# One-hots of a graph layer, made four tiles at a time with the tile as the inner dimension

## The chip, the cores and the metric

The kernel runs on one core of one Trainium2 chip. The metric is device microseconds of one execution, as the median of several runs; lower is better. Engines are called as the profile calls them: PE (TensorE matmul), PEld (TensorE weight load), DVE (VectorE), ACT (ScalarE), POOL (GpSimd) and SP (SyncE).

## The reference, cut to what matters

Two graph layers over 6250 nodes with 128 features and 106250 edges (100000 drawn, and one from each node to itself), sorted by `dst`:

```python
h = relu(layernorm(x));  x = x + L0(h)          # L0: degree-normalised sum over neighbours
h = relu(layernorm(x));  x = x + L1(h)          # L1: attention over the edges, by src
# L0
xw = h @ W;  deg = segment_sum(ones, dst);  dinv = rsqrt(deg)
out = relu(segment_sum(xw[src] * (dinv[src] * dinv[dst])[:, None], dst) + b)
# L1
att = exp(clip(sum_d(q[src] * k[dst]) / 4, -10, 10))     # 8 heads of 16
out = segment_sum(att * v[dst], src) / segment_sum(att, src);  layernorm(out + h) * gamma + beta
...
```

The first layer sums by `dst`, the order in which the edges come. The second one sums by `src`, so the kernel has to sort the edges by `src` on the chip, which it does beside the work of the first layer.

## The kernel before, in words

128 edges make a tile, one edge on each partition; there are `EC` = 831 tiles. Nodes are in `NB` = 49 blocks of 128.

**Head** (to about 110 us): layer norm of all nodes, degrees, `xw` scaled by `dinv`, written to the table `gtab`.

**First layer** (about 110 to 1065 us). The tiles come in groups of four (`G0`). For each group POOL gathers the rows of `gtab` by index (`gather`, L397, tile `gt`, 5 buffers), DVE makes a one-hot of the places within a window of 64 nodes (L923), PE sums by it (L952, `ps`), and DVE adds to `acc` (L934). When a block's edges are done, `finish0` adds, normalises and projects it. The first 16 blocks (`PC`) go another way: their edges are counted per pair of nodes, which gives a dense matrix `counts`, and `product` (L795) multiplies that with `xwp`, three bf16 parts of `xw`.

Between the groups stands the other work, by two lists of steps with written-out costs; `beside(k)` takes from each until its share for group k is spent. Engines then run their instructions in the order in which these were issued. The lists hold:

- `count_pair` (L756): two windows of 128 edges of the dense blocks. DVE compares a row of slot numbers with a code per edge, 245 columns (L769, `win_oh`, 4 buffers of a pair each), one instruction for each window. `put_counts` (L776) multiplies a pair two pairs later: 416 matmuls of 245 columns (L780), whose moving operand is `win_oh` and whose weights are `win_ol`; ACT copies the result (L783).
- the sort: keys, ranks (L550 to L553), positions; up to about 620 us.
- `place(t)` (L627), for each of the 831 tiles, about 623 to 1065 us: it puts the edges of tile t into their sorted places. DVE makes lane one-hots for 8 tiles at once, with the tiles as the inner dimension (`lanes`, L622 and L624, tile `ol`, 2 buffers). ACT scales one tile's lane one-hot (L641, `ola`, `LAG + 4` buffers); for one in four groups of 8, DVE does it (L635, `ola_v`). DVE compares slot numbers with a code, over the cells that tile t can reach (L643, `oh_tau`, `LAG + 4` buffers), one instruction per tile:

```python
oh = l0.tile([P, CELLS_IN * NB], F16, name="oh_tau", bufs=LAG + 4)
nc.vector.tensor_scalar(oh[:, :(hi + 1 - lo) * NB], self.slot16[:, lo * NB:(hi + 1) * NB],
                        r["code"][:, t:t + 1], None, op0=OP.is_equal)
```

`window(t)` gives the cells lo to hi; a cell is 49 columns. From its formula 133 tiles have one cell, 183 two, 116 three, 138 four, 200 five and 61 six. `put` (L650), `LAG` = 6 tiles later, multiplies: twice the tile's columns (weights `ol` and `ola`, moving operand `oh_tau`), in one or two pieces each (L656, `pp`).

- `unpack`, `rows_of` (L660, tile `lt`, 4 buffers) and flags, up to about 1105 us.

**Second layer** (from about 1110 us): attention over the sorted edges, block by block. The change doesn't touch it.

Of the kernel before, what the change touches and what calls it, by code (L numbers as in the profile page):

```python
# [7 lines left out]
F32 = mybir.dt.float32  # L8
F16 = mybir.dt.float16
BF16 = mybir.dt.bfloat16  # L10
I32 = mybir.dt.int32
# [3 lines left out]
OP = mybir.AluOpType  # L15
# [6 lines left out]
P = 128  # L22
D = 128
# [10 lines left out]
G1 = 3  # L34
BT = 16
PT = 8
LAG = 6
PC = 16
CN = 5
CW = -(-P // CN)  # L40
# [12 lines left out]
class Kernel:  # L53
# [31 lines left out]
    def setup(self, early):  # L85
        self.early = early
        nc, tc, ctx, NB, N = self.nc, self.tc, self.ctx, self.NB, self.N
# [7 lines left out]
        for name, a in (("dst", self.dstp), ("src", self.srcp)):  # L95
            t = self.nodes.tile([P, self.ER + 1], I32, name=f"{name}_i", tag=f"rows_{name}")
# [52 lines left out]
        nc.gpsimd.iota(pid_i, pattern=[[P, 2]], base=0, channel_multiplier=1)  # L149
        self.pid = const.tile([P, 2], F32, name="pid")  # L150
        nc.scalar.copy(self.pid, pid_i)
        NS = 1024
        slot_f = hp.tile([P, NS], F32, name="slot_f")
        nc.gpsimd.iota(slot_f, pattern=[[1, NS]], base=0, channel_multiplier=0,
                       allow_small_or_imprecise_dtypes=True)
# [2 lines left out]
        self.slot16 = const.tile([P, NS], F16, name="slot16")  # L158
        nc.scalar.copy(self.slot16, slot_f)

        self.lanes = self.nodes.tile([P, P, PT], F16, name="lanes")
        nc.scalar.copy(self.lanes, self.slot_f[:, :P, None].to_broadcast([P, P, PT]))

# [237 lines left out]
    def layer0(self):  # L401
        nc, tc, NB, NP, N, E, EC, ER, ET = self.nc, self.tc, self.NB, self.NP, self.N, self.E, self.EC, self.ER, self.ET
# [16 lines left out]
        with ExitStack() as l0c:  # L419
            l0k = l0c.enter_context(tc.tile_pool(name="l0k", bufs=1))  # L420
            l0 = l0c.enter_context(tc.tile_pool(name="l0", bufs=2))
            fin = l0c.enter_context(tc.tile_pool(name="fin", bufs=3))
# [61 lines left out]
            r = {}  # L484
# [118 lines left out]
            def window(t):  # L603
                per_tile = P * N / E
                d0, d1 = t * per_tile, (t + 1) * per_tile
                d0, d1 = d0 - 16 - 1.6 * d0 ** 0.5, d1 + 16 + 1.6 * d1 ** 0.5
                if d1 < PB * P:
                    return max(int(d0), 0) // (2 * P), int(d1) // (2 * P)
                share = (E - N) / N * P / N
                most = max(d1 - PB * P, 0) * share  # L610
                least = max(d0 - PB * P, 0) * share * min(1.0, self.LAST / P)
                hi = CELLS + min(int(most + 4.5 * most ** 0.5) // P, FAR - 1)
                if d0 < PB * P:
                    return max(int(d0), 0) // (2 * P), hi
                return CELLS + max(int(least - 4.5 * least ** 0.5), 0) // P, hi

            placed = []
            CELLS_IN = max(hi + 1 - lo for lo, hi in map(window, range(EC)))

            def lanes(t0, n):  # L620
                r["ol"] = l0.tile([P, 2, P, PT], F16, name="ol", bufs=2)
# [5 lines left out]
            def place(t):  # L627
                lo, hi = window(t)
                on_vector = t // PT % 4 == 3
                if t % PT == 0:  # L630
                    n = min(PT, EC - t)
                    lanes(t, n)
                    if on_vector:
                        r["ola"] = l0.tile([P, P, PT], F16, name="ola_v", bufs=1)
                        nc.vector.tensor_tensor(r["ola"][:, :, :n], r["ol"][:, 0, :, :n],  # L635
                                                r["a16"][:, None, t:t + n].to_broadcast([P, P, n]), op=OP.mult)
                if on_vector:
                    ola = r["ola"][:, :, t % PT]
                else:
                    ola = l0.tile([P, P], F16, name="ola", bufs=LAG + 4)  # L640
                    nc.scalar.activation(ola, r["ol"][:, 0, :, t % PT], AF.Copy, scale=r["a"][:, t:t + 1])  # L641
                oh = l0.tile([P, CELLS_IN * NB], F16, name="oh_tau", bufs=LAG + 4)
                nc.vector.tensor_scalar(oh[:, :(hi + 1 - lo) * NB], self.slot16[:, lo * NB:(hi + 1) * NB],  # L643
                                        r["code"][:, t:t + 1], None, op0=OP.is_equal)
                placed.append((t, lo, hi, oh, r["ol"], ola))
                if len(placed) > LAG:
                    put()
# [12 lines left out]
            def rows_of(table, what, c, m):  # L660
                pt, k = bank()
                nc.tensor.transpose(pt[:m, :P], what[:, c:c + m], self.ident)
                lt = fin.tile([P, P], BF16, name="lt", bufs=4)
                nc.scalar.copy(lt[:m, :], pt[:m, :P])
                let_go(k)
                nc.sync.dma_start(table[c:c + m, :], lt[:m, :])
# [60 lines left out]
            wins = {}  # L727

            def fetch_windows(q):
                rows = l0.tile([P, 2, P], I32, name="win", bufs=2)  # L730
                m = CQ * CW
                nc.gpsimd.indirect_dma_start(
                    out=rows[:m].rearrange("p a b -> p (a b)"), out_offset=None, in_=self.wins,
                    in_offset=bass.IndirectOffsetOnAxis(ap=self.win_row[:m, q:q + 1], axis=0))
                ints = l0.tile([P, 2, P], I32, name="win_int", bufs=1)
                nc.vector.tensor_scalar(ints[:m, 0, :], rows[:m, 0, :], 7, None, op0=OP.arith_shift_right)
                nc.vector.tensor_scalar(ints[:m, 1, :], rows[:m, 0, :], P - 1, None, op0=OP.bitwise_and)

                val = l0.tile([P, 2, P], F32, name="win_val", bufs=1)
                nc.vector.tensor_scalar(val[:m, 0, :], rows[:m, 1, :], self.win_node[:m, q:q + 1], float(NB),  # L740
                                        op0=OP.subtract, op1=OP.mult)
                nc.vector.tensor_tensor(val[:m, 0, :], val[:m, 0, :], ints[:m, 0, :], op=OP.add)
                nc.vector.tensor_copy(val[:m, 1, :], ints[:m, 1, :])
                pt, k = bank()
                for i in range(2):
                    nc.tensor.transpose(pt[:, i * P:i * P + m], val[:m, i, :], self.ident[:m, :m])
                code = l0.tile([P, P], F32, name="win_code", bufs=2)
                nc.scalar.copy(code[:, :m], pt[:, :m])
                lane = l0.tile([P, P], F16, name="win_lane", bufs=2)
                nc.scalar.copy(lane[:, :m], pt[:, P:P + m])  # L750
                let_go(k)
                wins[q] = [code, lane]

            counted = []

            def count_pair(b, j):  # L756
                q, m = b // CQ, CQ * CW
                code, lane = wins[q]
                w0 = b % CQ * CW + 2 * j
                oh = l0.tile([P, 2, 256], F16, name="win_oh", bufs=4)  # L760
                ols = []
                for h in range(2):
                    w = w0 + h
                    if w % PT == 0:
                        n = min(PT, m - w)
                        wins["ol"] = l0.tile([P, P, PT], F16, name="win_ol", bufs=2)
                        nc.vector.tensor_tensor(wins["ol"][:, :, :n], self.lanes[:, :, :n],
                                                lane[:, None, w:w + n].to_broadcast([P, P, n]), op=OP.is_equal)
                    nc.vector.tensor_scalar(oh[:, h, :CN * NB], self.slot16[:, :CN * NB], code[:, w:w + 1], None,  # L769
                                            op0=OP.is_equal)  # L770
                    ols.append(wins["ol"][:, :, w % PT])
                counted.append((j, oh, ols))
                if len(counted) > 2:
                    put_counts()

            def put_counts():  # L776
                j, oh, ols = counted.pop(0)
                cb = cbps.tile([P, 512], F32, name="cb")
                for h in range(2):
                    nc.tensor.matmul(cb[:, h * CN * NB:(h + 1) * CN * NB], ols[h], oh[:, h, :CN * NB], start=True,  # L780
                                     stop=True)
                c0 = 2 * j * CN
                nc.scalar.copy(self.counts[:, c0:c0 + 2 * CN, :].rearrange("p n b -> p (n b)"), cb[:, :2 * CN * NB])  # L783
# [60 lines left out]
            loads = {}  # L844

            def load0(b):
                own = fin.tile([P, D], F32, name="own", bufs=4)
                nc.sync.dma_start(own, gtab_v[:, b, :])
                xs = fin.tile([P, 1, D], F32, name="xs0", bufs=4)
                if b < NB - 1:  # L850
                    nc.sync.dma_start(xs[:, 0, :], self.x[b * P:(b + 1) * P, :])
                else:
                    nc.vector.memset(xs, 0.0)
                    nc.sync.dma_start(xs[:self.LAST, 0, :], self.x[b * P:N, :])
                loads[b] = own, xs
# [62 lines left out]
            ohs, sums, ats = {}, {}, {}  # L918
# [22 lines left out]
            for g in range(GA, self.NG0):  # L941
                n = size[g]
# [630 lines left out]
```

## Time and profile before

| what | value |
|---|---|
| median of 9 runs | 2329.36 us (2318.76 to 2342.37) |
| profiled execution, its own time | 2318.62 us |
| its span | 2316.8 us |
| PE, DVE, ACT, POOL busy | 73%, 67%, 43%, 52% |
| granted clock of PE, mean | 0.788 |

The profiled execution is one of the quicker ones: its own time is 10.7 us below the median. A stage is read as a stretch of the span; `win_oh` is made from 112.8 to 644.4 us, `oh_tau` from 623.0 to 1062.7 us. A mean duration counts an instruction from its start to its end; the next one on the same engine often starts before that, so the distance between starts is what an engine pays.

### The profile page before, as it was taken

The page shows a single profiled execution, that of the slowest core. Times are in us where ns is not written, and L with a number is a line of the kernel's source. Part 1 is how long each engine was busy: PE and PEld are TensorE (multiplying, and loading weights), DVE is VectorE, ACT ScalarE, POOL GpSimd, SP SyncE. Part 2 cuts the span into 40 slices and gives each one's busy share as a digit, 9 for nine tenths or more (in the row PEclk, how much of TensorE's full clock was granted, in tenths as well). Part 3 has the DMA queues.
Part 4 walks back from the last instruction along what each step waited for, and adds up shares of the span by engine and source line. Part 5 has one row for each costly group of instructions (what it writes and reads, how often), then busy time and mean ns, then how long its engine had stood idle before and what let it go on. Part 6 is the DMA issues. An engine that isn't in the chain of part 4 may idle for free.

```text
span 2316.8 us, 42149 instructions
## 1 busy us (share of the span) xinstructions
PE 1693.1 (73%) x14638; PEld 1440.2 (62%) x14638; DVE 1545.7 (67%) x4956; ACT 985.4 (43%) x2782; POOL 1193.8 (52%) x1173
## 2 busy tenths in 40 slices
PE   4335778877778888886448777777787777777777
PEld 4324667766666676565337666676676676676666
DVE  7822588778658888895236666567666667667667
ACT  6642443333347767772113343334334334334234
POOL 0575324554556666777455445454544554544550
PEclk9556787878765577996568788889888888888888
DMA  4411122222222222222634335334434434433440
GB/s 91 106 48 50 54 71 74 72 76 65 62 71 58 61 59 61 60 63 64 217 107 123 116 104 156 105 121 140 138 110 136 126 125 131 134 112 117 121 123 17
DMA packets 157205, 222.72 MB, mean 96 GB/s; under 512 B 30494, under 2 KB 115343, under 8 KB 156983
## 3 DMA queue, kind: packets, MB, share of 16 engines
q0 software_dynamic: 47488, 118.69, 18.0%
q1 hardware_dynamic: 103147, 98.05, 13.8%
q10 hardware_dynamic: 6348, 3.20, 0.7%
q8 instruction: 117, 1.92, 0.3%
q14 instruction: 105, 0.86, 0.1%
HBM read 192.44 MB, written 27.39 MB: 95 GB/s over the span
## 4 chain that ended last, share of the span: by engine, by line
PE 59%; issue 14%; DVE 9%; ACT 7%; another core or an unknown queue 5%; DMA 3%; POOL 1%; DVEq 0%; SPq 0%; ACTq 0%; POOLq 0%
PE po L1078 13%; PE pk L1036 11%; PE pq L1046 9%; PE cb L795 8%; PE pp L656 5%; PE ps L952 5%; PE ot L1050 3%; ACT ola L641 2%; PE cb L780 2%; DVE oh_tau L643 2%; ACT counts L783 2%; PE ps_f L890 1%; POOL gt L397 1%; DMA gt<-gtab,idx 1%
## 5 line engine op out<-in xcount | busy, mean ns | idle before, releaser
L397 POOL DMA_INDIRECT gt<-gtab,idx x567 | 609.6, 1075 | 491.2 <-issue 147.2
L397 POOL DMA_INDIRECT kv<-kvtab,idx x588 | 574.6, 977 | 558.6 <-DVE ohD L1029 173.6
L1046 PE MATMUL pq<-qb,ohT 128*128 128x128 bf16 x2940 | 262.3, 229 | 111.4 <-issue 106.7
L1036 PE MATMUL pk<-kvp,ohD 128*128 128x256 bf16 x2205 | 307.6, 293 | 24.5 <-issue 20.2
L1052 ACT COPY oh<-ot 128x384 f32<-128x384 f32 (+1 forms) x343 | 157.8, 463 | 353.7 <-PE pq L1046 98.1
L641 ACT ACTIVATE ola<-ol,a_f 128x128 f16<-128x128 f16 x624 | 272.1, 520 | 72.6 <-DVE ol L622 28.9
L1046 PEld LDWEIGHTS <-ohT 128*128 128x128 bf16 x2940 | 212.1, 103 | 138.2 <-issue 127.9
L952 PE MATMUL ps<-oh,gt 128*128 128x64 f32 x1134 | 216.9, 348 | 82.7 <-DVE acc L934 30.2
L1036 PEld LDWEIGHTS <-ohD 128*128 128x128 bf16 x2205 | 230.1, 105 | 71.8 <-issue 33.5
L952 PEld LDWEIGHTS ps<-oh,gt 128*128 128x128 f32 x1134 | 204.8, 265 | 92.0 <-issue 51.3
L795 PE MATMUL cb<-xwp,counts 128*128 128x128 bf16 x2352 | 194.0, 254 | 37.2 <-issue 28.4
L656 PE MATMUL pp<-oh_tau,ol 128*128 128x49 f16 (+5 forms) x947 | 198.5, 268 | 30.7 <-issue 11.6
L795 PEld LDWEIGHTS <-counts 128*128 128x128 bf16 x2352 | 187.5, 155 | 46.6 <-issue 39.1
L1058 DVE TENSOR_TENSOR pr<-pq,kv 128x384 f32<-128x384 f32 x196 | 108.6, 554 | 154.8 <-PE pk L1036 50.2
L643 DVE TENSOR_SCALAR oh_tau<-slot,code 128x245 f16<-128x245 f16 (+5 forms) x831 | 178.0, 277 | 24.2 <-PE pp L656 16.9
L1060 DVE TENSOR_REDUCE att<-pr 128x24 f32<-128x384 f32 x343 | 187.2, 546 | 0.1
L783 ACT CAST counts<-cb 128x490 bf16<-128x490 f32 x208 | 113.2, 570 | 169.5 <-PE cb L780 118.1
L1039 ACT COPY kvn<-pk 128x512 f32<-128x512 f32 (+1 forms) x245 | 115.6, 496 | 159.4 <-PE pq L1046 54.0
L1064 ACT ACTIVATE ex<-att 128x24 f32<-128x24 f32 x343 | 76.7, 224 | 228.8 <-DVE att L1062 152.6
L1029 DVE TENSOR_SCALAR ohD<-dr,pid 128x384 bf16<-128x384 bf16 (+1 forms) x294 | 81.6, 310 | 126.3 <-PE ot L1050 57.1
L656 PE MATMUL pp<-oh_tau,ola 128*128 128x98 f16 (+5 forms) x716 | 153.1, 261 | 15.6 <-issue 1.3
L1050 PE MATMUL ot<-identb,ohT 128*128 128x128 bf16 x980 | 125.8, 232 | 49.2 <-issue 41.9
(1766 smaller groups left out, 3131.7 us busy)
## 6 DMA issues: line engine op xcount, KB each, us to landing
lr<-lrow SPq DMA_DIRECT2D x48, 640.0 KB
dr<-drow SPq DMA_DIRECT2D x48, 256.0 KB
kv<-kvtab,idx POOLq DMA_INDIRECT x588
gt<-gtab,idx POOLq DMA_INDIRECT x567
kvtab<-kvout SPq DMA_DIRECT2D x49, 128.0 KB
kvn<-kvtab SPq DMA_DIRECT2D x49, 128.0 KB
qtab<-qp SPq DMA_DIRECT2D x49, 96.0 KB
qb<-qtab SPq DMA_DIRECT2D x48, 96.0 KB
```

Of the source, the lines that this page charges most:

```text
L397: self.nc.gpsimd.indirect_dma_start(out=to, out_offset=None, in_=table, in_offset=bass.IndirectOffsetOnAxis(ap=idx[:, t:t + 1], axis=0))
L641: nc.scalar.activation(ola, r["ol"][:, 0, :, t % PT], AF.Copy, scale=r["a"][:, t:t + 1])
L643: nc.vector.tensor_scalar(oh[:, :(hi + 1 - lo) * NB], self.slot16[:, lo * NB:(hi + 1) * NB], r["code"][:, t:t + 1], None, op0=OP.is_equal)
L656: nc.tensor.matmul(pp[:, h, (x0 - f0) * NB:(x1 - f0) * NB], o, oh[:, (x0 - lo) * NB:(x1 - lo) * NB], start=False, stop=t == EC - 1, skip_g ...
L783: nc.scalar.copy(self.counts[:, c0:c0 + 2 * CN, :].rearrange("p n b -> p (n b)"), cb[:, :2 * CN * NB])
L795: nc.tensor.matmul(prods[b][:, :D], self.counts[:, :P, k], self.xwp[:, k, x, :], start=(k, x) == (0, 0), stop=(k, x) == (NB - 1, 2))
L952: nc.tensor.matmul(ps, gt[:, j, :], oh[:, j, :], start=(j == 0), stop=(j == n - 1))
L1036: nc.tensor.matmul(pk[:, i - c, :], ohD[:, h, i * P:(i + 1) * P], kvp[:, 2 * tiles[i] + h, x, :], start=(h, x) == mine[0], stop=(h, x) == ...
L1046: nc.tensor.matmul(pq[:, i * D:(i + 1) * D], left, qb[:, x * D:(x + 1) * D], start=(x == 0), stop=(x == 2))
L1050: nc.tensor.matmul(ot[:, i, :], ohT[:, i * P:(i + 1) * P], identb, start=True, stop=True)
L1060: nc.vector.tensor_reduce(att[:, :n * H], pr[:, :n, :].rearrange("p g (h d) -> p (g h) d", h=H), axis=AX.X, op=OP.add)
L1078: nc.tensor.matmul(po, left, wv_[:, i, :], start=(k == 0 and i == 0), stop=(k == len(steps) - 1 and i == n - 1))
```

## The change

Both wide one-hots are made for `PW` = 4 tiles by one comparison of two tensors. The constant `wide` holds each slot number four times side by side; the tile is the inner dimension of the result, so that one tile's columns stand 4 f16 elements (8 bytes) apart. That strided view is now the moving operand of the matmuls. For the places, the codes are first made relative to the first cell of the four tiles (`rel_code`), whose cells are the union of the four windows. `LAG` goes from 6 to 4 (so `ola` has 8 buffers), and some pools have fewer buffers (`lt`, `win`, `own`, `xs0`), which makes room in SBUF.

```diff
-LAG = 6
+PW = 4
+LAG = 4
...
+        self.wide = self.nodes.tile([P, CW5, PW], F16, name="wide")
+        nc.scalar.copy(self.wide, slot_f[:, :CW5, None].to_broadcast([P, CW5, PW]))
...
-                oh = l0.tile([P, CELLS_IN * NB], F16, name="oh_tau", bufs=LAG + 4)
-                nc.vector.tensor_scalar(oh[:, :(hi + 1 - lo) * NB], self.slot16[:, lo * NB:(hi + 1) * NB],
-                                        r["code"][:, t:t + 1], None, op0=OP.is_equal)
+                if t % PW == 0:
+                    n = min(PW, EC - t)
+                    r["lo"], last = window(t)[0], window(t + n - 1)[1]
+                    cols = (last + 1 - r["lo"]) * NB
+                    rel = l0.tile([P, PW], F16, name="rel_code", bufs=3)
+                    nc.vector.tensor_scalar(rel[:, :n], r["code"][:, t:t + n], -float(r["lo"] * NB), None, op0=OP.add)
+                    r["oh"] = l0.tile([P, CELLS_IN * NB, PW], F16, name="oh_tau", bufs=3)
+                    nc.vector.tensor_tensor(r["oh"][:, :cols, :n], self.wide[:, :cols, :n],
+                                            rel[:, None, :n].to_broadcast([P, cols, n]), op=OP.is_equal)
+                oh = r["oh"][:, (lo - r["lo"]) * NB:(hi + 1 - r["lo"]) * NB, t % PW]
...
-                lt = fin.tile([P, P], BF16, name="lt", bufs=4)
+                lt = fin.tile([P, P], BF16, name="lt", bufs=2)
...
-                rows = l0.tile([P, 2, P], I32, name="win", bufs=2)
+                rows = l0.tile([P, 2, P], I32, name="win", bufs=1)
...
+                nc.vector.tensor_scalar(val[:m, 0, :], val[:m, 0, :], -1.0, 1024.0, op0=OP.max, op1=OP.min)
...
-                code = l0.tile([P, P], F32, name="win_code", bufs=2)
+                code = l0.tile([P, P], F16, name="win_code", bufs=2)
...
-                oh = l0.tile([P, 2, 256], F16, name="win_oh", bufs=4)
...
-                    nc.vector.tensor_scalar(oh[:, h, :CN * NB], self.slot16[:, :CN * NB], code[:, w:w + 1], None,
-                                            op0=OP.is_equal)
+                    if w % PW == 0:
+                        n = min(PW, m - w)
+                        wins["oh"] = l0.tile([P, CN * NB, PW], F16, name="win_oh", bufs=2)
+                        nc.vector.tensor_tensor(wins["oh"][:, :, :n], self.wide[:, :CN * NB, :n],
+                                                code[:, None, w:w + n].to_broadcast([P, CN * NB, n]), op=OP.is_equal)
+                    ohs.append(wins["oh"][:, :, w % PW])
...
-                    nc.tensor.matmul(cb[:, h * CN * NB:(h + 1) * CN * NB], ols[h], oh[:, h, :CN * NB], start=True,
+                    nc.tensor.matmul(cb[:, h * CN * NB:(h + 1) * CN * NB], ols[h], ohs[h], start=True,
...
-                own = fin.tile([P, D], F32, name="own", bufs=4)
+                own = fin.tile([P, D], F32, name="own", bufs=3)
-                xs = fin.tile([P, 1, D], F32, name="xs0", bufs=4)
+                xs = fin.tile([P, 1, D], F32, name="xs0", bufs=3)
```

## The prediction

> **What bounds the kernel now.** I read the chain of waits by stages first, then the busy time by stages. The chain from 183 to 623 us (counts, products, sort) lists PE L795 at 39.4%, L780 at 7.7% and L952 at 8.7%, and DVE's L769 at 3.1%. From 860 to 1065 us (the wide places) it lists PE L656 at 32.9%, and on DVE L643 at 14.8% and L622 and L624 at 7.4% and 6.4%.
>
> ```profile
> 183.00:623.00 440.00, 335.24 (x2990) 286.65 (x2991) 302.94 (x947) 166.10 (x414) 207.51 (x199) 0.78 0.24 66
> 623.00:860.00 237.00, 191.53 (x1585) 156.85 (x1583) 176.65 (x714) 156.97 (x388) 148.96 (x139) 0.60 0.23 62
> 860.00:1065.00 205.00, 172.84 (x1202) 125.95 (x1202) 181.28 (x680) 146.30 (x358) 146.08 (x130) 0.89 0.22 60
> ```
>
> The columns are length, busy PE, PEld, DVE, ACT, POOL, granted clock, DMA share, GB/s. In the last stage DVE is busy 88% and PE 84%: two engines stand near their end. The change takes work from DVE, and gives PE another way of reading. So the price of both has to be found, by bursts in the timeline and by the tiles' rows:
>
> ```profile
> 43.15 1.73 PE L289 MATMUL ps_b<-hi,lo 128*128 128x49 f16 x16
> 1002.98 1.53 DVE L643 TENSOR_SCALAR oh_tau<-slot,code 128x294 f16<-128x294 f16 x7
> 856.80 1.28 DVE L643 TENSOR_SCALAR oh_tau<-slot,code 128x147 f16<-128x147 f16 x7
> 720.49 1.10 DVE L643 TENSOR_SCALAR oh_tau<-slot,code 128x49 f16<-128x49 f16 x7
> L289 PE MATMUL ps_b<-hi,lo x96: 253/280/287, 43.2 to 58.5; 128*128 128x49 f16 x96
> L282 DVE TENSOR_TENSOR hi<-lanes,nblk x6: 561/567/569, 40.2 to 53.0; 128x784 f16<-128x784 f16 x6
> L286 DVE TENSOR_TENSOR lo<-lanes,nlane x6: 1218/1220/1222, 40.7 to 53.5; 128x2048 f16<-128x2048 f16 x6
> L656 PEld LDWEIGHTS <-ol x947: 140/146/277, 633.5 to 1064.3; 128*128 128x128 f16 x190
> L656 PEld LDWEIGHTS <-ola x716: 95/104/258, 633.7 to 1062.0; 128*128 128x128 f16 x179
> L780 PE MATMUL cb<-win_oh,win_ol x416: 265/268/428, 113.4 to 646.2; 128*128 128x245 f16 x139
> ```
>
> The first line is the one to look at: in the head, `hi` is a moving operand whose columns stand 16 f16 elements (32 bytes) apart, the only such matmul before the change.
>
> **DVE, places.** A burst of seven takes its length less the last one's duration, over six: 0.14 us each at 49 columns ((1.10-0.24)/6), 0.17 at 147, 0.21 at 294. Tiles have 3.33 cells (163 columns) in the mean, so 831 x 0.17 = 141 us. New: 208 comparisons. The rows of `hi` and `lo` give (1220-567)/(2048-784) = 0.517 ns per element; `ol` with 1024 elements starts at 1004.43 and the next instruction at 1005.03, 0.60 us, which leaves 0.07 us fixed. The unions have 705 cells in all, 664 elements each in the mean: 208 x (0.07 + 0.34) = 86 us. Before each stands a `rel_code` of 4 elements; the reciprocal L173 (one element) gives way after 0.07 us (855.90 to 855.97), so 208 x 0.07 = 15 us; in the built order another instruction mostly stands between it and its reader, otherwise it is up to 0.23 us (855.90 to 856.13) or 48 us. Sum 101 us: DVE loses 40 us (7 to 43), little of it at five and six cells (5 cells: 4 x 0.19 = 0.76 becomes 0.58 + 0.07), more where windows are narrow.
>
> **DVE, counts.** 416 x 0.19 = 79 us (245 columns give way to the next after 0.19 us, 1008.63 to 1008.82) become 104 x (0.07 + 980 x 0.517 ns) = 60 us: 19 us less, in a stage where L769 is 3% of the chain.
>
> **PE, the strided moving operand.** This term decides. Packed columns cost 0.43 ns: 49 columns start to end in 183 ns at the least, 245 in 268 at the median, 85 ns for 196 more. At 32 bytes apart, 16 matmuls in 1.73 us with 0.28 for the last are 97 ns each for 49 columns, 2.0 ns per column. Could that be the weights' load? `ol` is loaded with columns 16 bytes apart in 146 ns against 104 packed, and L795's weights, 98 bytes apart, take 155 ns, yet its matmuls follow each other in 64 to 65 ns. So strided weights explain 65 ns and not 97; the moving operand does the rest. The weights also show that the price is full at 16 bytes and no higher at 98: it is one price per fetch, which packed columns share. At 8 bytes, two columns lie in 16 bytes. The bounds are 0.43 and 2.0 ns per column; I take half of the far row, 1.0, since two columns would share a fetch.
>
> "Advanced Engine Details and Errata" of the Trainium skill, section Memory Cachelines, speaks against that: SBUF lines have 16 bytes, and two hits on a line are enough to absorb the latency of the access. By it 8 bytes would cost PE nothing, and the sum would be the first rival's. No run here shows two hits per line.
>
> At half the clock a packed column costs 0.83 already, so the extra is columns x (1.0 - 0.417/clock). Places multiply 271 thousand columns (twice the windows). By stretches of 80 us, with their clocks (0.68, 0.50, 0.63, 0.81, 0.94, 0.92) and an even pace of tiles, the extra is 8, 4, 15, 29, 42 and 25 us, 123 in all. Counts have 102 thousand: 43 us.
>
> **What lies on the path.** From 860 to 1065 us PE must do: 182 thousand columns at 1.0 ns, 182 us; 33 groups of L952 at 1.0 to 1.1 us, 35; six or seven blocks' transposes and projections at about 2.5 us, 17. That is 234 to 250 us in a stretch of 205, so PE alone sets the end and DVE's saving drops out: +40. From 623 to 860 us 27 us more PE meets 25 us less DVE, with the clock at 0.60 and both at 75 to 81%: 0. From 183 to 623 us the extra 43 us count by PE's share of those lines and of what queues behind them, 41%: +17. DVE's 19 us there at 3% of the chain: 0.
>
> **Small parts.** `wide` is 1176 elements on ACT at about 18 us; `lanes` with 1024 took 1039 ns, so 1.2 us ahead of the first h0 of a head whose chain then runs through ACT and PE: +1. The clamp in `fetch_windows`, 4 x 0.2 us, lies beside gathers: 0; uncovered, 1. The loads of `own` and `xs0` are issued a block (some 20 us) ahead, so a buffer less costs nothing; SP's queue has no compute behind it. `lt` with 2 buffers: copies are 2.7 us apart (12 in 32 us) and a store has two such distances to land; if it fails, the next copy on ACT waits, up to 1 us x 12, while POOL's gathers set the pace there: 0. `LAG` 4: `put(t)` stands two tiles earlier in PE's order, in front of the group's L952, and ACT may lead PE by 8 tiles and not 10. PE waits for `ola` 35.3 us now (121 times). At worst 67 groups x 2 tiles x 0.42 us = 56 us; `oh_tau`'s 12 buffers against 10 work the other way. With PE as the bound ACT is ahead anyway: 0.
>
> Sum: 40 + 0 + 17 + 1 = +58 us. Against the profiled execution's own time, 2318.6 becomes 2377; on the median, 10.7 higher, 2329.4 becomes 2387.
>
> **Rivals.**
> 1. Faster: PE reads 8 bytes apart at the packed rate. Then DVE's 40 us count where DVE is the limit. From 860 to 1065 us about 12 to 17 us come off a queue that is 88% busy; of the 25 us before, half, since PE and ACT are waited for as well; 3 of the counts' 19. About -25 us, 2304 (2285 to 2318). For it: DVE's burst lines stand end to end from 1002 to 1012 us, and DVE is on the chain with L643 at 14.8%. Against: the row of L289. It decides below about 0.75 ns per column: there PE in the last stage needs 182 x 0.75 + 52 = 189 us, what DVE would leave (205 - 15).
> 2. Much slower: the full 2.0 ns per column. PE in the last stage needs 182 x 2.0 + 52 = 416 us, +211; from 623 to 860 us 76 thousand columns add some 100 us to PE's 174, +35; counts 145 x 0.41 = +60: 2635. Against: two neighbours within the stretch that the weights' rows point to.
> 3. No change: a column between 0.6 and 0.8 ns, or packed rate with the shorter `LAG` and fewer buffers taking back the 25 us by ACT's and DVE's waits for PE: 2320 to 2341.
>
> **Chances.** My case (0.8 to 1.2 ns per column, 2345 to 2430) 0.54; rival 1 0.28; rival 3 0.11; rival 2 0.07. Half a per cent, 11.6 us, is about what a measurement can tell from none. Faster by more: rival 1 but for its weak end, and a little of 3: 0.28. Same: 0.12. Slower: 0.60. The range takes in my case with its upper bound and rival 1 down to 2298, leaving out rival 2, the lower third of rival 1 and a rest: 2298 to 2435. The likeliest case alone, 2345 to 2430.
>
> **What would show it.** Right: L780 with 245 columns rises from 268 ns to some 400, and L656 in bursts from 0.105 us per 245 columns to about 0.25; DVE's busy share from 860 us on falls below 75% while PE stands above 90%, and `ol` and `oh_tau` wait for PE `pp`. L643 is replaced by 208 comparisons of 0.2 to 0.75 us. Wrong: L780 stays at 268 ns and the last stage shortens (rival 1); it rises above 600 (rival 2); or PE's bursts are unchanged and PEld's wait for ACT `ola` grows beyond 35 us (rival 3).

## The result, and the profile after

The median went from 2335.57 us (62 runs) to 2405.39 us (19 runs): 1.029 times, 95% interval 1.027 to 1.031, 70 us slower. The prediction was +58 us, 2387, in a range up to 2435. The profiled execution of the changed kernel has a span of 2397.2 us and an own time of 2399.01 us, at the same mean granted clock as before (0.788).

In the changed kernel the counts' comparison is L783 and its matmul L795, the product L810; the places' comparison is L653, the lane one-hots L626 and L628, the placing matmul L667, the group's matmul L967. First the busy time by stages (length, PE, PEld, DVE, ACT, POOL, granted clock, DMA share, GB/s), as of before; the last stage is longer now, so it is cut in two:

```profile
183.00:623.00 440.00, 348.27 (x2886) 282.14 (x2884) 279.77 (x650) 162.99 (x406) 196.80 (x189) 0.77 0.22 64
623.00:860.00 237.00, 176.41 (x1406) 151.43 (x1405) 135.93 (x459) 141.27 (x351) 141.23 (x135) 0.59 0.22 61
860.00:1040.00 180.00, 156.59 (x1026) 119.09 (x1026) 123.52 (x350) 111.47 (x268) 100.70 (x96) 0.82 0.18 50
1040.00:1131.00 91.00, 90.35 (x436) 56.38 (x435) 67.59 (x178) 57.82 (x138) 54.03 (x49) 1.00 0.19 52
```

DVE, busy 88% of the last stage before, is at 69% and 74%; PE, 84% before, is at 87% and then 99%. The chain of waits from 860 to 1131 us says the same: PE's placing matmuls have 68.2% of it (32.9% before), and DVE's `oh_tau`, 14.8% before, has 1.0%.

```profile
by line: PE pp L667 68.2%; PE ps L967 12.9%; issue 6.6%; PE ps_f L905 2.7%; ACT ola L645 1.7%; DVE ol L626 1.2%; POOL gt L400 1.1%; DVE oh_tau L653 1.0%; another core or an unknown queue 1.0%; DVE ol L628 0.9%; PE ps_f L901 0.7%; PE ps_f L9
```

The tiles' rows give each operation's price (minimum/median/maximum in ns, first and last start in us). The third line stood at 265/268/428 before. The last line is the idle time of the engines ahead of the instructions that read or write `ol`, until PE's placing matmuls let them go on: 101.6 us in 74 waits, 19.3 us in 20 before. Of it 48.0 us are DVE's (8.9 before) and 53.6 us ACT's, which makes `ola` from `ol` (9.5 before).

```profile
L667 PE MATMUL pp<-oh_tau,ol x947: 206/278/449, 650.6 to 1131.1; 128*128 128x98 f16 x54, 128*128 128x49 f16 x51, 128*128 128x245 f16 x41, 128*128 128x196 f16 x22
L653 DVE TENSOR_TENSOR oh_tau<-wide,rel_code x208: 232/467/772, 633.0 to 1126.5; 128x980 f16<-128x980 f16 x26, 128x392 f16<-128x392 f16 x23, 128x784 f16<-128x784 f16 x17, 128x196 f16<-128x196 f16 x15
L795 PE MATMUL cb<-win_oh,win_ol x416: 378/398/432, 113.6 to 666.3; 128*128 128x245 f16 x139
L783 DVE TENSOR_TENSOR win_oh<-wide,win_code x104: 633/668/727, 112.9 to 659.3; 128x980 f16<-128x980 f16 x104
  PE pp L667: 101.6, 74
```

A matmul's duration has a fixed part (the shortest of 947 takes 206 ns, while those with 98 columns follow each other in 90), so the distance between starts in bursts is the better measure: 219 to 220 ns for 245 columns of `oh_tau`, 175 for 196, 90 for 98, that is 0.89 to 0.92 ns per column. It is the same where the granted clock is 0.5 and where it is 1.0; the packed 245 columns of before took 105 ns at full clock and some 206 at half.

Where the 80 us between the two spans lie, by starts in both traces (us):

| step | before | after | difference |
|---|---|---|---|
| first placing matmul | 633.7 | 650.6 | +17 |
| from it to the 975th placing matmul | 224.6 | 240.8 | +16 |
| from there to the last one | 206.3 | 239.9 | +34 |
| from there to the last gather for the first layer | 43.7 | 41.6 | -2 |
| from there to the second layer's first matmul | 26.0 | 34.7 | +9 |
| second layer | 1182.4 | 1189.6 | +7 |

The medians differ by 70 and not 80, as the profiled execution of before is one of the quicker ones.

### The profile page after: what moved, and what is told of

It reads as the page before. It is cut to its first block, busy times and chain, and to the rows that moved or that the text cites. A ratio compares the mean times of both kernels' runs of the same rounds, so it can differ in the third digit from the quotient of the medians.

```text
span 2397.2 us, 41686 instructions
## 1 busy us (share of the span) xinstructions
PE 1774.8 (74%) x14638; PEld 1481.3 (62%) x14638; DVE 1486.8 (62%) x4233; ACT 991.2 (41%) x2783; POOL 1185.1 (49%) x1173
## 4 chain that ended last, share of the span: by engine, by line
PE 60%; issue 14%; DVE 7%; another core or an unknown queue 7%; ACT 7%; DMA 3%; POOL 1%; DVEq 0%; SPq 0%; ACTq 0%; POOLq 0%
PE po L1093 12%; PE pk L1051 10%; PE pp L667 9%; PE pq L1061 8%; PE cb L810 8%; PE ps L967 5%; PE ot L1065 3%; PE cb L795 2%; PE ps_f L905 2%; ACT counts L798 2%; DMA gt<-gtab,idx 2%; POOL gt L400 1%; DMA xs<-in_x_dram 1%; ACT ola L645 1%
## 5 line engine op out<-in xcount | busy, mean ns | idle before, releaser
L400 POOL DMA_INDIRECT gt<-gtab,idx x567 | 599.4, 1057 | 558.8 <-PE ps L967 266.8
L1051 PE MATMUL pk<-kvp,ohD 128*128 128x256 bf16 x2205 | 319.2, 299 | 25.5 <-issue 24.8
L645 ACT ACTIVATE ola<-ol,a_f 128x128 f16<-128x128 f16 x624 | 276.6, 518 | 126.6 <-PE pp L667 53.6
L1051 PEld LDWEIGHTS <-ohD 128*128 128x128 bf16 x2205 | 235.4, 107 | 79.1 <-issue 37.1
L667 PE MATMUL pp<-oh_tau,ol 128*128 128x49 f16 (+5 forms) x947 | 250.3, 311 | 38.4 <-DVE oh_tau L653 29.8
L967 PE MATMUL ps<-oh,gt 128*128 128x64 f32 x1134 | 209.3, 339 | 93.6 <-DVE acc L949 58.8
L967 PEld LDWEIGHTS ps<-oh,gt 128*128 128x128 f32 x1134 | 205.5, 259 | 108.5 <-DVE acc L949 62.6
L810 PE MATMUL cb<-xwp,counts 128*128 128x128 bf16 x2352 | 199.2, 255 | 68.1 <-issue 62.1
L810 PEld LDWEIGHTS <-counts 128*128 128x128 bf16 x2352 | 189.8, 155 | 81.1 <-issue 73.0
L667 PE MATMUL pp<-oh_tau,ola 128*128 128x98 f16 (+5 forms) x716 | 191.5, 310 | 15.7 <-issue 7.4
L667 PEld LDWEIGHTS <-ol 128*128 128x128 f16 x947 | 134.9, 153 | 41.6 <-issue 6.4
```

The lines of the kernel that those rows point to most:

```text
L400: self.nc.gpsimd.indirect_dma_start(out=to, out_offset=None, in_=table, in_offset=bass.IndirectOffsetOnAxis(ap=idx[:, t:t + 1], axis=0))
L667: nc.tensor.matmul(pp[:, h, (x0 - f0) * NB:(x1 - f0) * NB], o, oh[:, (x0 - lo) * NB:(x1 - lo) * NB], start=False, stop=t == EC - 1, skip_g ...
L810: nc.tensor.matmul(prods[b][:, :D], self.counts[:, :P, k], self.xwp[:, k, x, :], start=(k, x) == (0, 0), stop=(k, x) == (NB - 1, 2))
L967: nc.tensor.matmul(ps, gt[:, j, :], oh[:, j, :], start=(j == 0), stop=(j == n - 1))
L1051: nc.tensor.matmul(pk[:, i - c, :], ohD[:, h, i * P:(i + 1) * P], kvp[:, 2 * tiles[i] + h, x, :], start=(h, x) == mine[0], stop=(h, x) == ...
```

## The experiments

They ran on other chips, on which the kernel before takes about 1773 us instead of 2336: its second layer takes 793 us there instead of 1182, and begins at 979 us instead of 1134. So each is compared with the kernel before on its own chip. Where a stage is named, these are starts in the traces: "placing stretch" is the first to the last placing matmul, "tail" the last gather of the first layer to the second layer's first matmul.

### What a column costs

A small kernel by itself. PE multiplies 48 times the same 245 columns, whose distance in the tile is 1, 2, 3, 4, 6, 8, 16 and 32 f16 elements, then 49 packed columns with weights at distances of 1 to 49.

```diff
+for s in (1, 2, 3, 4, 6, 8, 16, 32):
+    m = pool.tile([P, 245, s], F16)          # moving operand m[:, :, 0]
+    for i in range(48):
+        matmul(pt[:, :245], packed, m[:, :, 0])
```

> The disputed price by itself: bursts of 48 matmuls of 245 columns each (f16) with packed weights, the moving operand's columns 1, 2, 3, 4, 6, 8, 16 and 32 elements apart, then bursts of 48 of 49 packed columns with weights 1, 2, 4, 8, 16 and 49 elements apart, then 49 columns with steps 4 and 16 under weights of step 16 and 1. Nothing of the reference is computed. Theory 'shared fetch' (a fetch brings 16 bytes and takes about 1.8 to 2.0 ns, columns within it share it): per matmul 0.105 us at step 1 and 2, 0.21 to 0.25 at step 4, 0.43 to 0.49 at steps 8, 16 and 32 alike. Rival 'word' (a fetch brings 4 bytes in 0.83 ns): 0.105 at step 1, 0.205 at steps 2, 3, 4, 6, and more from 8 on only if something else adds. Rival 'weights' (the 97 ns of L289 were the weights' load): steps 4 to 32 all near 0.105 with packed weights. Weights: about 25 ns per matmul at step 1, 60 to 70 at steps 8, 16, 49; under the shared fetch about half of that surplus at step 4.

The timeline of PE shows the bursts at distances 4, 8 and 16, with one or two matmuls of the neighbouring burst in each row (start, length, count):

```profile
45.17 10.93 PE L36 MATMUL pt<-mv,packed 128*128 128x245 f16 x50
71.13 21.59 PE L36 MATMUL pt<-mv,packed 128*128 128x245 f16 x50
92.11 21.79 PE L36 MATMUL pt<-mv,packed 128*128 128x245 f16 x49
```

The first row divided is 10.93/50 = 0.219 us for each matmul, just what the changed kernel pays; the second 0.43, the third 0.44. By the median distance of starts, for all distances:

| elements apart | 1 | 2 | 3 | 4 | 6 | 8 | 16 | 32 |
|---|---|---|---|---|---|---|---|---|
| ns for 245 columns | 105 | 111 | 163 | 219 | 326 | 433 | 441 | 412 |
| ns per column | 0.43 | 0.45 | 0.66 | 0.89 | 1.33 | 1.77 | 1.80 | 1.68 |

The row of the burst at 16 elements was taken at a granted clock of 0.50, that at 4 elements at 1.00:

```profile
45.40:56.00 10.60, 10.60 (x51) 5.62 (x50) 0.28 (x1) 0.00 (x0) 1.00 0.00 0
92.40:113.60 21.20, 21.20 (x49) 6.06 (x48) 0.28 (x1) 0.00 (x0) 0.50 0.00 0
```

It is about 1.77 ns for every 16 bytes, shared by the columns that lie in them: one column at 8 elements pays it all, two at 4 half of it, four at 2 a quarter, which is the packed rate at full clock (part of the burst at 2 ran at half the clock and took 206 ns there, as packed columns do). 49 packed columns with weights 1, 2, 4, 8, 16 and 49 elements apart take 25, 25, 33, 60, 62 and 65 ns, the last two at a granted clock of 0.50; at 4 elements some 45 were expected. Last, 49 columns 16 elements apart take 91 ns with packed weights and 98 with weights 16 apart, which is the head's row of 97 ns. So that row was nearly all the moving operand's, as the prediction had it, and half of it was the right rule, with 0.89 for 1.0.

### What the stride costs in the kernel

The changed kernel with its matmuls reading packed columns of the same tiles. These are other columns, and indices are cut to 4095, so only the first layer is read; the second one gathers other rows, which its 2101 us hold.

```diff
-oh = r["oh"][:, (lo - r["lo"]) * NB:(hi + 1 - r["lo"]) * NB, t % PW]
+oh = r["oh"].rearrange("p c t -> p (c t)")[:, (lo - r["lo"]) * NB:(hi + 1 - r["lo"]) * NB]
...
-ohs.append(wins["oh"][:, :, w % PW])
+ohs.append(wins["oh"].rearrange("p c t -> p (c t)")[:, w % PW * CN * NB:(w % PW + 1) * CN * NB])
```

> The changed kernel with all of its DVE work, buffers and LAG, but the matmuls of both one-hots read as many packed columns of the same tile instead of the strided ones. So wrong columns are multiplied; the sorted places are wrong, indices are kept within 4096 and the flag that chooses the general path is fixed, so that the rest of the kernel runs as before. Theory 'stride' (the whole loss is PE's strided read): the packed matmul of 245 columns is back at 0.105 us apart, and the time falls to the first rival's world, 2300 to 2325 us, 10 to 35 below the kernel before. Rival 'slack' (LAG 4, fewer buffers and four-at-once bursts make the loss): the time stays at 2380 to 2405. In between, the shares are read off.

The counts' matmul is back at the price of before, so only the read had changed it:

```profile
L798 PE MATMUL cb<-win_oh,win_ol x416: 265/272/428, 112.9 to 543.5; 128*128 128x245 f16 x139
```

The placing stretch is 362 us. With the strided read it is 397 us on the same chip (places only, below) and 399 in the changed kernel: the strided read costs 35 to 37 us there. `ola` and `oh_tau` are back on the chain of waits from 700 to 897 us with 12.4% and 11.0%, and `pp` has 22.4%. The placing matmuls' rows, packed read and then changed kernel:

```profile
L669 PE MATMUL pp<-oh_tau,ol x947: 183/249/414, 535.0 to 896.9; 128*128 128x98 f16 x54, 128*128 128x49 f16 x51, 128*128 128x245 f16 x41, 128*128 128x196 f16 x22
L667 PE MATMUL pp<-oh_tau,ol x947: 206/278/451, 543.6 to 942.3; 128*128 128x98 f16 x54, 128*128 128x49 f16 x51, 128*128 128x245 f16 x41, 128*128 128x196 f16 x22
```

The changed kernel and the kernel before, on one chip:

> The kernel before, unchanged, for a profile from the chip on which the experiments ran, whose time for it is 1773 us and not 2336. Both theories expect nothing new of it but the marks to compare with: counts and products that end at about 540 us (as with the places alone changed, 543), places that take about 390 us (as with the counts alone changed, 389), and a second layer of about 790 us, in which the engines' common idle stretches of 2 to 8 us are missing.

> The changed kernel, unchanged, on the chip of the experiments. Stride theory with DVE's gain: counts' one-hots cost about what they did alone, 21 us at the end of the products, and places 8 us (35 for the strided read less 27 that DVE's saving brings with a packed read), together 1800 to 1810 us. If the two parts hide each other: 1785 to 1795.

The marks of the kernel before were not where they were expected: the products end at 558.3 us and the places take 374.7 us. It takes 1772.4 us there (9 runs), the changed one 1811.38: 1.0224 (1.0193 to 1.0255), 39 us. Its placing stretch is 398.9 us against 374.7: the first 975 matmuls take 180.3 against 185.7 (5 us less), the rest 218.6 against 189.0 (30 us more). The chain of waits from 724 to 942 us in the changed kernel there:

```profile
by line: PE pp L667 78.8%; PE ps L967 12.2%; PE ps_f L905 2.7%; DVE ol L626 1.3%; ACT ola L645 1.0%; DVE oh_tau L653 0.8%; issue 0.6%; PE ps_f L906 0.6%; PE ps_f L901 0.5%; PE ps_f L884 0.4%; DVE ol L628 0.3%; DVE ola_v L639 0.3%; ACT hs L8
```

PE sets the end of the wide places there, as the prediction had it.

One trace of each kernel divides the loss (us from the start; the packed read has all of the change but the stride, and ran on another of these chips than the two others):

| | before | packed read | changed |
|---|---|---|---|
| first product | 164.4 | 159.0 | 158.5 |
| last product | 558.3 | 555.2 | 563.2 |
| first placing matmul | 541.3 | 535.0 | 543.6 |
| last gather for the first layer | 958.5 | 950.8 | 981.4 |
| tail | 20.5 | 30.9 | 30.9 |

Up to the last gather the strided read costs 31 us, 9 of them by the first placing matmul. Without it the change would be 8 us ahead there, part of which is the earlier first product. The tail is 10 us longer with either read, so it is another matter than the stride.

### One half of the change at a time

Both keep `LAG` 4 and the small buffers; the first one has the places as in the changed kernel and the counts as before, the second the other way round.

```diff
 # places only: counts back to
+nc.vector.tensor_scalar(oh[:, h, :CN * NB], self.slot16[:, :CN * NB], code[:, w:w + 1], None, op0=OP.is_equal)
 # counts only: places back to
+nc.vector.tensor_scalar(oh[:, :(hi + 1 - lo) * NB], self.slot16[:, lo * NB:(hi + 1) * NB],
+                        r["code"][:, t:t + 1], None, op0=OP.is_equal)
```

> The changed kernel with the counts' one-hots made as before (one comparison per window, packed). Theory 'stride': the counts' share of the loss goes: of 70 us about 17 to 23, so 2380 to 2388. If the counts were hidden behind the products: 2400 to 2405.

> The changed kernel with the places' one-hots made as before (one comparison per tile, packed), but LAG 4 and all the smaller buffer counts kept. Theory 'stride': the places' share of the loss goes, about 50 us, so 2350 to 2358. Rival 'slack': LAG 4 and the buffers keep much of it, 2370 or more.

Places only: 1784.2 us, 1.0058 (1.0039 to 1.0076), placing stretch 397.1. Counts only: 1803.57 us, 1.0174 (1.0149 to 1.02), placing stretch 389.0. They don't add up to the whole change: 11 and 31 us, against 39 with the common part in both. The products of places only end at 542.6 us, some 20 us ahead of most other kernels with small buffers (563 us and more, 555 with the packed read), since its first product runs at 146.6 us and not at 157 or later; why its start is quicker was not found. So this pair can't be used for a sum, only the placing stretches can. But counts only has most of the loss without any strided read in the places. That pointed to what both halves share.

### What both halves share: LAG and buffers

The kernel before with nothing but the five smaller numbers:

```diff
-LAG = 6
+LAG = 4
-lt = fin.tile([P, P], BF16, name="lt", bufs=4)
+lt = fin.tile([P, P], BF16, name="lt", bufs=2)
-rows = l0.tile([P, 2, P], I32, name="win", bufs=2)
+rows = l0.tile([P, 2, P], I32, name="win", bufs=1)
-own = fin.tile([P, D], F32, name="own", bufs=4)
+own = fin.tile([P, D], F32, name="own", bufs=3)
-xs = fin.tile([P, 1, D], F32, name="xs0", bufs=4)
+xs = fin.tile([P, 1, D], F32, name="xs0", bufs=3)
```

> The kernel before with LAG 4 and the smaller buffer counts alone (lt, win, own, xs0; win_oh stays), all one-hots as before. Stride theory: no difference that can be measured, ratio 0.996 to 1.005. Slack theory: much of the 31 us that the counts alone seemed to cost (with LAG 4 in it) comes from here, so 1785 to 1800.

1797.03 us, 1.0136 (1.0111 to 1.0162): 25 us, with no wide one-hot at all. The prediction had this at 0. But the 25 us can't be taken out of the 39 us of the whole change: the packed read has these numbers too and reaches the last gather before the kernel before does. In it only the longer tail is left of them. Three kernels take the numbers apart:

```diff
 # lag only
-LAG = 6
+LAG = 4
 # buffers only: lt 2, win 1, own 3, xs0 3, LAG 6
 # win only: win 1
```

> The kernel before with LAG 4 instead of 6 and nothing else (ola 8 buffers, oh_tau 8; lt, win, own, xs0 as before). LAG 4 and fewer buffers together cost 24 us over the kernel before (1772 us). Theory LAG: the shorter distance between a one-hot and its matmul makes PE wait for ola and oh_tau, and puts the placing matmuls of two tiles ahead of the group's own matmul; then this kernel is slower by 15 to 25 us, with the placing matmuls' stretch at 384 us or more instead of 375. Rival, buffers: the placing stretch stays within 3 us of 375 us and the time within 8 us of the kernel before. Rival, both: 8 to 15 us slower.

> The kernel before with lt 2, win 1, own 3 and xs0 3 buffers, LAG 6 as before. Theory LAG: within 8 us of the kernel before; products end within 2 us of 558 us. Rival, buffers: 15 to 25 us slower, with the products ending at 561 us or later and the stretch from the last placing matmul to the second layer's first one 66 us or more instead of 63. Rival, both: 8 to 15 us slower.

> The kernel before with win 1 buffer instead of 2, all else as before. One gather of the windows then waits for the unpacking of the last one on POOL's queue, in front of the groups' gathers, until the products are made. If that is the term: 5 us or more slower, products ending 3 us or more later than 558 us. If not: within 3 us of the kernel before, and what the smaller buffers cost lies in lt, own and xs0.

| kernel | time | ratio | products end | placing stretch | tail |
|---|---|---|---|---|---|
| before (one trace) | 1774.0 | | 558.3 | 374.7 | 20.5 |
| lag only | 1783.05 | 1.0052 (1.0037 to 1.0067) | 558.1 | 385.2 | 20.2 |
| buffers only | 1790.05 | 1.0084 (1.0053 to 1.0115) | 566.3 | 373.3 | 28.0 |
| win only | 1779.84 | 1.0027 (1.0013 to 1.0042) | 565.4 | 375.0 | 20.2 |
| all of them | 1797.03 | 1.0136 (1.0111 to 1.0162) | 562.9 | 385.5 | 27.8 |

The table has a place for each: `LAG` costs some 10 us in the placing stretch, `lt`, `own` and `xs0` some 8 us in the tail, `win` some 7 us ahead of the end of the products (5 us of the time). By the ratios it is 9 us for `LAG` and 15 for the buffers, 24 of the 25.

`LAG`: with eight `ola` and eight `oh_tau` buffers instead of ten, the producers wait for PE. For ACT, ahead of `ola`, the kernel before shows no wait for `pp` there; in lag only (us, times):

```profile
  PE pp L656: 11.6, 5
```

and DVE, ahead of `oh_tau`, waits 11.6 us in 13 waits for `pp` instead of 3.5 us in 6. DVE is busy for 347 of the 375 us of the placing stretch in the kernel before, so it has little room for waits: its idle time there grows from 28 to 36 us, which is most of the 10. That is this layout. In the changed kernel `oh_tau` has room for 12 tiles, and DVE is idle for 85 of the 399 us (busy 314). What `LAG` costs there was not run.

`lt`, `own` and `xs0`: SP's queue at the end of the first layer. First the kernel before, then buffers only (start, length):

```profile
930.51 0.42 SPq L848 DMA_DIRECT2D own<-gtab  x1
936.42 7.49 SPq L666 DMA_DIRECT2D drow<-lt  x3
```

```profile
948.72 6.67 SPq L666 DMA_DIRECT2D drow<-lt  x3
964.89 0.32 SPq L881 DMA_DIRECT2D xtab<-xs  x1
965.30 0.29 SPq L666 DMA_DIRECT2D drow<-lt  x1
965.64 0.33 SPq L848 DMA_DIRECT2D own<-gtab  x1
```

With a buffer less, the load of the last block's `own` no longer stands ahead of the stores of an earlier block but behind `xtab` from `xs`, which waits for an earlier block's arithmetic; it is issued at 965.6 us instead of 930.5. The last store of `lt` is behind it too, at 965.3 instead of 943. What follows in the queue, the last blocks' loads and the stores that the second layer reads, comes later. For the last block's `xs0` DVE then waits (us, times); the kernel before has no such wait:

```profile
  DMA xs<-in_x_dram: 3.5, 1
```

The rest of the 8 us must come from elsewhere. The last blocks were late before that load: the `lt` copies take 26 us there and 18 in the kernel before (13 to 26 in the others with 4 buffers), and the add for the fourth block from the end, which follows the last of them, comes 16 us later. Kernel before, then buffers only:

```profile
L664 ACT CAST lt<-ps_f x12: 254/265/285, 925.1 to 943.3; 128x128 bf16<-128x128 f32 x10, 84x128 bf16<-84x128 f32 x1, 8x128 bf16<-8x128 f32 x1
945.15 0.29 DVE L870 TENSOR_TENSOR own<-own,ps_f 128x128 f32<-128x128 f32 x1 [0.20 <-PE ps_f L869]
```

```profile
L664 ACT CAST lt<-ps_f x12: 243/266/283, 931.6 to 957.3; 128x128 bf16<-128x128 f32 x10, 84x128 bf16<-84x128 f32 x1, 8x128 bf16<-8x128 f32 x1
961.61 0.29 DVE L870 TENSOR_TENSOR own<-own,ps_f 128x128 f32<-128x128 f32 x1 [0.20 <-PE ps_f L869]
```

So `lt` can be a cause as well as the two loads. Lag only and win only, with these buffers at 4, have the tail of before. Which of `lt`, `own` and `xs0` does it was not tried.

`win`: the gather of the last windows goes out behind 152 gathers of POOL's queue instead of 80. Its first and last start, and DVE's wait for it, in win only:

```profile
L732 POOL DMA_INDIRECT win<-in_wins_dram,win_row_c x4: 974/977/1052, 107.1 to 333.0; - x4
  DMA win<-in_wins_dram,win_row_c: 15.6, 2
```

In the kernel before the last one starts at 187.6 us and the wait is 7.2 us, once. That fits 5 us, but the products were already 5 us late at 214 us, before that gather, in a stretch (165 to 300 us) where the granted clock was 0.78 instead of 0.83. So the mechanism of these 5 us stays open.

### Four bytes apart

Two tiles at once and not four; codes in f16, no `rel_code`, `LAG` 4, the small buffers, counts as before.

```diff
+PW = 2
...
-oh = l0.tile([P, CELLS_IN * NB], F16, name="oh_tau", bufs=LAG + 4)
-nc.vector.tensor_scalar(oh[:, :(hi + 1 - lo) * NB], ...
+r["oh"] = l0.tile([P, CELLS_IN * NB, PW], F16, name="oh_tau", bufs=4)
+nc.vector.tensor_tensor(r["oh"][:, :cols, :n], self.wide[:, r["lo"] * NB:(last + 1) * NB, :n],
+                        r["code"][:, None, t:t + n].to_broadcast([P, cols, n]), op=OP.is_equal)
```

> The places' one-hots made for 2 tiles at once, with the tile as the inner dimension: the moving operand's columns are 4 bytes apart, which the bursts of the step experiment showed at 0.45 ns per column, as good as packed. The comparison is with the whole row of slot numbers, each held twice, so that no code relative to the first cell is needed. LAG 4 and the smaller buffer counts as in the run with these alone; counts as before. Theory shared fetch: matmuls of 245 columns stay at 105 to 111 ns, a comparison for two tiles of five cells takes 0.07 + 490 x 0.517 ns = 0.32 us against 2 x 0.19, one for two tiles of one cell 0.12 against 0.29, so DVE loses some 40 us in the places and they end 15 to 30 us sooner: 1745 to 1765. If a run of two elements costs DVE its pace (one element per 1.04 ns), a comparison takes 0.58 us, and the time rises to 1790 or more.

1809.13 us, 1.0189 (1.0166 to 1.0213), far from the 1745 to 1765 expected. The prices are not why: the matmuls are back at packed prices (median 253 ns for those with `ol`, 267 in the kernel with the small numbers alone), and DVE's comparisons follow each other in 0.32 us for 490 elements, the price expected:

```profile
L650 DVE TENSOR_TENSOR oh_tau<-wide,code x416: 177/313/469, 543.8 to 926.4; 128x490 f16<-128x490 f16 x34, 128x196 f16<-128x196 f16 x32, 128x392 f16<-128x392 f16 x22, 128x98 f16<-128x98 f16 x21
```

The placing stretch falls to 374.1 us, 11 below that of the small numbers alone. Yet the kernel is 12 us slower than that one: it starts its counts some 6 us later, and from the last placing matmul to the last gather it takes 58 us instead of 40. What those 18 us are, the next experiment shows.

### Wide one-hots for narrow tiles only

`LAG` and all buffers as before, in the room of tiles that are dead by then; wide one-hots only for groups of four tiles that reach at most two cells; counts as before.

```diff
+r["narrow"] = last + 1 - r["lo"] <= 2
+if r["narrow"]:
+    r["oh"] = ...name="oh_wide", tag="ti", bufs=3        # the tensor comparison of the change
+else:
+    oh = l0.tile([P, CELLS_IN * NB], F16, name="oh_tau", bufs=LAG + 4)   # as before
```

> The kernel before, with the wide one-hots only for those groups of four tiles that reach at most two cells (98 columns), about the first third of the places; LAG 6 and all buffers as before, since wide, oh_wide lie in the room of tiles that are dead by then (win and ti); counts as before. From the rows: four packed comparisons of 98 columns cost DVE about 0.62 us, one wide one with its rel_code 0.34; PE pays 0.45 ns more for each of some 62 thousand columns at full clock and nothing at half. Theory: DVE's and ACT's queue paces the narrow tiles and LAG and buffers were what spoilt the gain; then the stretch from the first placing matmul to the 975th is 172 to 180 us instead of 186, and the time 6 to 14 us below the kernel before (1773 us). Rival, the strided read eats it there too: the stretch stays at 184 us or more and the time within 4 us of the kernel before. The step from the last gather of the first layer to the second layer's first matmul should be 20 us as in the kernels with all buffers, not 28.

1772.81 us, 0.9996 (0.9978 to 1.0014): no difference. The first 975 placing matmuls take 176.0 us instead of 185.7, as expected, and the placing ends at 903.5 us instead of 916.0. The tail is 21 us, that of full buffers. But the last gather comes at 953.5 instead of 958.5: of 12.5 us that the placing gains, 5 are left. Busy times from the end of the placing to the last gather, narrow only and the kernel before:

```profile
903.00:953.00 50.00, 31.31 (x129) 23.79 (x127) 19.62 (x68) 6.68 (x25) 38.11 (x40) 0.60 0.27 75
916.00:958.00 42.00, 26.92 (x124) 21.13 (x122) 19.03 (x66) 6.68 (x25) 32.02 (x33) 0.62 0.30 79
```

The fifth number is POOL. It issues gathers end to end, one every 1.25 us, and has 40 left when the placing is done, instead of 34. So most of what the placing gains is given back to POOL's queue.

In the kernel before that queue has no room either. Here are POOL's waits for the placing matmuls in its placing stretch (us, times, longest), and then the same on the chip of the result:

```profile
POOL gt L397 <- PE pp L656: 15.3, 48, 0.8
```

```profile
POOL gt L397 <- PE pp L656: 63.1, 42, 9.7
```

On the chips of the experiments POOL issues 297 gathers from the first placing matmul to the last gather, in 417 us, mostly 0.3 us apart and never more than 0.8. In narrow only it takes 414 us for them, with the packed read 416. In the kernel with pairs no gap is over 0.3 us, but a gather takes 1187 ns in the placing stretch, against 1117 in the kernel before: 46 are left there at the end of the placing, and all 297 take 432 us. Why they take longer was not tried. So as long as gathers take what they take, no saving in the places alone shortens the first layer by much on these chips. On the chip of the result POOL waited up to 9.7 us, so it is not shown for that one.

## Why the prediction was right, and where it was not

- **DVE: right in size.** It was priced at 40 and 19 us less; the page's DVE goes from 1545.7 to 1486.8 us, 59 less. The 208 comparisons have 0.23 to 0.77 us (named: 0.2 to 0.75).
- **The strided column: the rule right, the size close.** The term that decides was 1.0 ns per column, half of the far row; it is 0.89. The counts' matmul is at 398 ns (named: some 400), the bursts of 245 columns at 0.22 us (0.25). By 0.89 the extra PE time would be 93 and 32 us instead of 123 and 43; PE's busy time rose by 82 us in all, less than the two together.
- **The rule that spoke against it.** By "Advanced Engine Details and Errata" of the Trainium skill, section Memory Cachelines, two hits on a line of 16 bytes absorb the latency. Here two hits cost PE 0.89 ns per column and four 0.45, against 0.43 packed. For a moving operand the measurement decides: two are not enough. With that the first rival (PE reads at the packed rate, 2304 us) falls, and the second (2.0 ns, 2635) as well.
- **The last stage: right.** PE was to need 234 to 250 us in a stretch of 205; it took 240 (+34, predicted +40), PE busy up to 99% with DVE and ACT waiting for it. On the other chip it was +30. The packed read shows there that the stride does it: 362 instead of 399 us for the placing.
- **The counts: right as a sum, not shown as a mechanism.** The first placing matmul was to be 17 us late and was 17 us late. But the share of 41% is no sum of the rows that the prediction shows (L795 and L780 have 47.1% together). On the other chips the strided read costs 8 or 9 us there, but the changed kernel is only 2 us late (543.6 against 541.3), and its first product is 6 us early. What the stride takes in the counts on the first chip is not known by itself.
- **The step that failed: the buffers at 0.** Fewer buffers were priced at nothing, with SP's idle queue as their cover ("SP's queue has no compute behind it"). They cost 15 us by themselves on the other chips, 8 of them in the tail of the first layer. Every kernel with the smaller `lt`, `own` and `xs0` has a tail of 27 to 31 us there, every other one 20 or 21. The tail's +9 on the first chip is of that size.
- **`LAG` at 0: open.** In the kernel before it costs 9 us on the other chips, where DVE has little room for waits. The prediction's reason ("With PE as the bound ACT is ahead anyway") is about the changed kernel, where no run shows what it costs. The 56 us that the prediction gave as the worst case were not reached.
- **From 623 to 860 us: 0 predicted, +16 measured.** This stays open, as on the other chip the changed kernel is 5 us quicker there.

So the direction and the main mechanism held, as far as the other chips can show it: there 31 us of the first layer come and go with the strided read, and the tail is 10 us longer. The sum, 58 for 70, came out somewhat low. That it is so near is partly luck: the two profiled executions differ by 80 us, and in them 16, 9 and 7 us stand where the prediction had 0. How the 70 us divide on the first chip was not measured there; the second layer's +7 in the two traces has no explanation either.

## What to carry to other kernels

Before a one-hot is laid out with the tiles inside, count how many columns of one tile share 16 bytes: four (2 tiles in f16) are read by PE at the packed price, two (4 tiles) at twice it, and at a low granted clock the difference hides. Price the smaller numbers that make room for a change as edits of their own, and read for each the order of every queue, SP's too. And ask which queue stays as it is: on the chips of the experiments POOL's gathers take back most of what the places gain.

## What was not expected of the hardware

- A strided read costs PE the same at a granted clock of 0.5 and of 1.0 (0.219 us for 245 columns at 4 elements), while a packed one doubles; so at half the clock the stride is nearly free (0.84 ns packed, 0.89 strided).
- At 3 and 6 elements the price lies between, 0.66 and 1.33 ns: it goes with the share of 16 bytes, not with whole steps.
- The same kernel takes 2336 us on one chip and 1773 on others. In the chain of waits of the whole span "issue" has 14.5% on the first and 2.2% on one of the others; what it stands for was not looked into.
